# An attention-and-graph kernel on one core: the products with adj moved to stand behind the second block of queries, a pair's blocks dealt out anew among its four attention units, and the norms asked for one step sooner

## The chip, the core and the metric

The kernel runs on one core of a Trainium2 chip. The metric is the device time of one execution in microseconds (us). Before the change the median of three runs is 2553.65 us (2553.41 to 2556.24). The profile describes one execution with a span of 2553.1 us. The granted TensorE clock in it was 0.995 of full speed, so the clock plays no part in what follows.

## The reference

The input x has 64 graphs of 256 nodes with 512 features; adj is one 256 x 256 matrix of zeros and ones. Two layers follow each other, each a residual with a layer norm behind it:

```
def _L0_gnn_ref(x, adj, Wq, bq, Wk, bk, Wv, bv, Wo, bo):        # H = 8 heads of HD = 64
    q, k, v = (x @ W + b).reshape(b, n, H, HD) for each of the three
    scores = jnp.einsum('bqhd,bkhd->bhqk', q, k) / jnp.sqrt(jnp.float32(HD))
    scores = scores + (1.0 - adj)[None, None, :, :] * -1000000000.0
    attn = jax.nn.softmax(scores, axis=-1)
    out = jnp.einsum('bhqk,bkhd->bqhd', attn, v).reshape(b, n, d)
    return out @ Wo + bo
def _L1_gnn_ref(x, adj, weight, bias):
    y = jnp.einsum('nm,bmd->bnd', adj, x)
    return jnp.einsum('bnd,do->bno', y, weight) + bias

x = _layernorm(x + _L0_gnn_ref(x, adj, ...))
x = _layernorm(x + _L1_gnn_ref(x, adj, ...))
```

## The kernel before, in words

**Tiles.** The 64 graphs are worked through in 32 pairs. For each pair there are five large products with a 512 x 512 weight matrix: v, q and k (the values, queries and keys of attention), o (attention's output times Wo) and l (the second layer's output times its weight). Each is cut into four *blocks* of 128 x 512 (j = 0 to 3). To get float32-like accuracy from faster matmuls, both operands are split into three parts (high, low and a difference), and a block is three part products of four matmuls each. `near` (L317) does the first two parts into a PSUM bank and has ScalarE scale what stands there (L326); `far` (L328) does the third part later and has the bank emptied: for v, q, k by ScalarE (L347, L352), for o and l by VectorE, which adds it to the residual rows r (L338). There are four banks for these products (`ps_mm`, four buffers), and `LAGGED` (L522) holds the blocks that have had `near` but not `far`; `block` (L532) leaves at most two of them open, and the step `f1` or `f0` in the order below closes all but one, or all.

**Splitting the operands.** On VectorE, `chunk_parts` (L284) makes the parts of one 128-row chunk of the input of o or l: cut (L168), clow (L169) and cdiff (L174); ScalarE makes chigh from cut (L298). `x_t`, `x_parts` and `x_diff` (L240 to L274) do the same for the rows of x of a later pair, in xT, x, low and diff.

**Attention.** A pair has four *units*: two graphs times two groups of four heads. One `slot` (L580) finishes one unit and begins the next: `values` (L384) does row sums (L394) and attention times v (L402), which ScalarE takes out of PSUM as zc (L396) and vc (L405); `scores` (L359) does q times k for the next unit in two halves (kc = 0 and 1, L367), and ScalarE takes the exponential (L371). The PSUM tiles `at` of a slot are six, in a ring of four buffers: the second half of the scores goes into the buffers of zc's and vc's inputs.

**The products with adj.** `adj_x` (L501) multiplies adj with the normed rows; there are four for a pair (y0 to y3). Its input comes out of a chain: when `far` of o's last block has run, `norm` (L433) begins; ScalarE squares the rows (`squared`, L442), VectorE and GpSimd make the inverse roots (L446), VectorE makes `less` (L465), ScalarE norms the rows (`normed`, L476), and `halves` splits them into two parts hl on ScalarE and VectorE (L498, L499). The rows of the second layer pass through the same norm and go out to DRAM.

**What sets the order.** In the middle of the kernel (windows 1 to 30, one for each pair) the order of the instructions on TensorE, ScalarE and VectorE is exactly the order in which the Python code issues them (`manual_schedule`). `between` (L540) writes the large steps of a window by hand as one list, `seq`. The small steps of the norm chain are put off by `later(n, ...)` (L225): they are issued after n further *ticks*, and a tick comes after every block, slot and adj product (L591). In a window w, the blocks of o and l belong to the pair behind (w - 1), those of v, q and k to the pair ahead (w + 1), and the slots to the pair w. A window takes 77.4 us; this document calls its four slots S1 (which opens the window), S2, S3 and S4.

Of the kernel before, what the change touches and what calls it, by code (L numbers as in the profile page):

```python
# [43 lines left out]
def fast(tc, x, adj, wq, bq, wk, bk, wv, bv, wo, bo, w1, b1, out):  # L44
# [6 lines left out]
    NP = B // 2  # L51
# [78 lines left out]
    def raw_weight(name, tiles, queue):  # L130

        for i in range(3):
            SCRATCH[name, i] = scratch.tile([P, DC, D], F32, name=f"{name}{i}")
        n = DC // len(tiles)
        for i, t in enumerate(tiles):
            for k in range(n):
                RAW[name, i * n + k] = t[:, k]
            w = SOURCE[name][i * n * P:(i + 1) * n * P]
            if name == "o":


                for a in range(n):
                    queue.dma_start(t[:, a], w.rearrange("(h a i) e -> a h i e", h=4, a=2)[a])
            else:
                queue.dma_start(t, w.rearrange("(c p) e -> p c e", p=P))
# [79 lines left out]
    def later(n, f, *args):  # L225
        due.append([n, f, args])
# [101 lines left out]
    def far(name, p, j):  # L328
        pm = BANKS.pop((name, p, j))
        if (name, p, 2) in WP:  # L330
            part_product(pm, name, p, j, 2)
        b, c = divmod(j, 2)
        if name in "ol":
            r = R[p][b][:, c]
            if p < NP - 2:
                if j == 0:
                    ST[p, name] = small.tile([P, 4], F32, name="sums")
                nc.vector.scalar_tensor_tensor(r, pm, 1.0, r, op0=OP.mult, op1=OP.add, accum_out=ST[p, name][:, j:j + 1])  # L338
                if j == 3:
                    norm(p, name)  # L340
            else:
                nc.vector.tensor_tensor(r, r, pm, op=OP.add)
                norm_tile(p, name, j)
        elif name == "v":
            if c == 0:
                V[p, b] = four.tile([P, NC, D], F32, name="v")
            nc.scalar.activation(V[p, b][:, c], pm, AF.Copy)  # L347
        else:
            T, bias = (K, bk_s) if name == "k" else (Q, bq_s)
            if c == 0:  # L350
                T[p, b] = qk.tile([P, 2, 2, N], F32, name=name + "T")
            nc.scalar.activation(T[p, b][:, c].rearrange("p b i -> p (b i)"), pm, AF.Identity, bias=bias[:, j:j + 1])  # L352
# [80 lines left out]
    def norm(p, name):  # L433

        mean = small.tile([P, 4], F32, name="mean")
        nc.vector.tensor_scalar(mean, ST.pop((p, name)), -1 / D, None, op0=OP.mult)  # L436
        squares = small.tile([P, 4], F32, name="squares")
        for j in range(4):
            later(1 + j // 2, squared, p, j, mean, squares)
        later(3, inverse_roots, p, name, mean, squares)  # L440

    def squared(p, j, mean, squares):  # L442
        waste = one.tile([P, D], mybir.dt.bfloat16, name="z")
# [2 lines left out]
    def inverse_roots(p, name, mean, squares):  # L446
        nc.vector.tensor_scalar(squares, squares, 1 / D, EPS, op0=OP.mult, op1=OP.add)
        rstd = small.tile([P, 4], F32, name="rstd")
        nc.gpsimd.tensor_tensor(rstd, squares, power, op=OP.pow)
        later(1, less_of, p, name, 0, mean, rstd)  # L450

    def norm_tile(p, name, j):
        st = small.tile([P, nc.vector.BN_STATS_DIM], F32, name="st")
        nc.vector.bn_stats(st, R[p][j // 2][:, j % 2])
        mv = small.tile([P, nc.vector.BN_AGGR_DIM], F32, name="mv")
        nc.vector.bn_aggr(mv, st)
        ve = small.tile([P, 1], F32, name="ve")
        nc.vector.tensor_scalar(ve, mv[:, 1:2], EPS, None, op0=OP.add)
        rstd = small.tile([P, 1], F32, name="rstd1")
        nc.gpsimd.tensor_tensor(rstd, ve, power[:, 0:1], op=OP.pow)  # L460
        mean = small.tile([P, 1], F32, name="mean1")
        nc.vector.tensor_scalar(mean, mv[:, 0:1], -1.0, None, op0=OP.mult)
        later(1, less_of, p, name, j, mean, rstd)

    def less_of(p, name, j, mean, rstd):  # L465

        n = rstd.shape[1]
        less = small.tile([P, n], F32, name=f"less{n}")
        nc.vector.tensor_tensor(less, mean, rstd, op=OP.mult)  # L469
        for i in range(n):  # L470
            later(1 + i, normed, p, name == "l", j + i, rstd[:, i:i + 1], less[:, i:i + 1])

    def normed(p, layer, j, rstd, less):
        b, c = divmod(j, 2)
# [65 lines left out]
    def between(w):  # L540

        ahead, behind = w + 1, w - 1
        b = lambda name: [(block, name, behind if name in "ol" else ahead, j) for j in range(4)]
        v, q, k, o, l = (b(n) for n in "vqkol")
        c = lambda name, p: [(chunk_parts, name, p, j) for j in range(4)]
        y = [(adj_x, behind, i) for i in range(4)]
        bo_steps = [(with_bo, w, b) for b in range(2)]
        x_steps = [(x_t, w + 2, i) for i in range(4) if w + 2 < NP]
        x1 = [[s for f in (x_t, x_parts) for s in [(f, w + 2, i)] if w + 2 < NP] for i in range(4)]
        x2 = [[(x_diff, w + 2, i)] if w + 2 < NP else [] for i in range(4)]  # L550
        slot, f1 = [None], [(caught_up, 1)]
        f0 = [(caught_up,)]
        split = lambda name: [(split_w, name, i) for i in range(4)]
        mixed = lambda m, n: [s for pair in zip(m, n) for s in pair]
        halves_tiles = lambda: [one.tile([P, 2, D], F32, name=f"hl{i}") for i in range(2)]
        if w == -1:
            return [(x_t, 0, i) for i in range(4)] + mixed(v, split("v")) + mixed(q, split("q")) + [(adj_t,)] + \
                mixed(k, x_steps)
        if w == 0:
            raw_weight("o", halves_tiles(), nc.sync)  # L560
            PENDING[:] = [s for m, n in zip(x1, x2) for s in m + n]
            return slot + mixed(v, split("k")) + slot + q[:3] + split("o") + [(bv_wo,), (load_w, 3)] + \
                [(lambda: raw_weight("l", halves_tiles(), nc.sync),)] + slot + q[3:] + k[:2] + split("l") + \
                [(load_r, 0)] + slot + k[2:] + bo_steps + c("o", w)[:2] + \
                [(load_w, 3), (load_r, 1)]
        co, cl = c("o", behind), c("l", behind)
        seq = slot + co[2:3] + o[:1] + f1 + co[3:] + o[1:2] + PENDING[:6] + o[2:] + PENDING[6:] + slot + v + q[:1] + slot + q[1:] + f1 + \
            y[:1] + f0 + y[1:2] + k[:1] + (cl[:1] if w < NP - 2 else []) + y[2:] + f0 + bo_steps + slot + k[1:2] + \
            (cl[1:2] if w < NP - 2 else [])
        PENDING[:] = x1[3] + x2[3]  # L570
        if w == NP - 2:
            co = c("o", w)
            return seq + k[2:3] + co[:1] + k[3:] + co[1:2] + [(block, "o", w, 0)] + cl[:1] + [(block, "o", w, 1)] + cl[1:2]
        seq += k[2:3] + cl[2:3] + k[3:] + x1[0] + l[:1] + f1 + x2[0] + x1[1] + x2[1] + l[1:2] + cl[3:] + \
            l[2:3] + c("o", w)[:1] + x1[2] + x2[2] + l[3:] + f1 + c("o", w)[1:2]
        return seq

    PENDING = []
# [16 lines left out]
    def window(w):  # L595
        steps(between(w), [(w - 1, 3)] + [(w, u) for u in range(4)])
# [235 lines left out]
```

## Time and profile before

| engine | busy us | share of the span |
|---|---|---|
| TensorE (PE), matmuls | 2496.0 | 98% |
| TensorE weight loads (PEld) | 1886.6 | 74% |
| VectorE (DVE) | 1872.6 | 73% |
| ScalarE (ACT) | 1705.7 | 67% |
| GpSimd (POOL) | 382.4 | 15% |

Windows 2 to 29 repeat to within 0.02 us: the longest pieces of the chain of waits begin at 222.88, 300.26, 377.62, 455.00 us and so on, 77.38 us apart. In one such window (996.62 to 1074.00 us) TensorE is busy for 76.74 us, VectorE for 57.49 us and ScalarE for 53.09 us.

How to read a timeline: each line is one or more instructions of one engine with the start and the length in us, the line of the kernel, what it writes from what it reads, and in brackets the time that the engine stood idle ahead of it and what ended that. Matmuls overlap: four of them show as 1.07 us, but the next group starts 0.91 us after the first one did.

### The profile page before, as it was taken

What the parts mean: (1) busy time and instruction counts of PE and PEld (TensorE: products, weight loads), DVE (VectorE), ACT (ScalarE), POOL (GpSimd) and SP (SyncE); (2) the same over time, 40 slices, a digit from 0 to 9 for tenths busy, and PEclk for the clock granted to TensorE, in tenths of its full rate; (3) what the DMA queues carried; (4) which work ended last, traced back from release to release, by engine and by line L of the source; (5) the groups of instructions that cost most, each with busy time, mean ns of one, the idle gap of its engine ahead of it and who ended that gap; (6) DMA issues with size and microseconds to landing.
All of it is one profiled execution on the core that took longest, in us unless ns stands there. A gap on an engine that the chain in (4) does not pass through costs nothing.

```text
span 2553.1 us, 42184 instructions
## 1 busy us (share of the span) xinstructions
PE 2496.0 (98%) x15806; PEld 1886.6 (74%) x15806; DVE 1872.6 (73%) x3239; ACT 1705.7 (67%) x3206; POOL 382.4 (15%) x793
## 2 busy tenths in 40 slices
PE   8999999999999999999999999999999999999997
PEld 4477777777777777777777777777777777777765
DVE  4676787677886677876767876768876778866786
ACT  4557666776666766666776667766667766677755
POOL 0111111111111111111111111111111111111101
PEclk9999999999999999999999999999999999999998
DMA  7868778778788687777787787787787787777711
GB/s 205 284 201 273 235 232 259 240 244 243 240 256 247 236 263 232 235 250 252 231 274 226 232 259 243 240 262 234 246 246 247 251 247 233 247 254 229 257 68 51
DMA packets 375744, 600.25 MB, mean 235 GB/s; under 512 B 273520, under 2 KB 273776, under 8 KB 317552
## 3 DMA queue, kind: packets, MB, share of 16 engines
q0 software_dynamic: 65232, 475.03, 51.9%
q1 hardware_dynamic: 309760, 121.42, 22.0%
q8 instruction: 127, 2.08, 0.3%
q10 hardware_dynamic: 544, 1.05, 0.1%
q14 instruction: 81, 0.66, 0.1%
HBM read 548.15 MB, written 49.28 MB: 234 GB/s over the span
## 4 chain that ended last, share of the span: by engine, by line
PE 70%; DVE 25%; issue 3%; DMA 1%; ACT 0%; POOL 0%; SPq 0%; DVEq 0%; ACTq 0%
PE mm L314 50%; PE at L367 7%; PE at L402 6%; PE mm L512 5%; DVE clow L169 4%; DVE r L338 3%; DVE cdiff L174 3%; DVE diff L174 2%; DVE cut L168 2%; PE at L394 2%; DVE e L376 2%; DVE low L169 2%; DVE xT L264 2%; DVE x L168 1%; DVE o L418 1%
## 5 line engine op out<-in xcount | busy, mean ns | idle before, releaser
L326 ACT ACTIVATE mm<-mm 128x512 f32<-128x512 f32 x616 | 357.8, 581 | 356.7 <-PE mm L314 356.6
L376 DVE TENSOR_TENSOR e<-e,adjT 128x1024 f32<-128x1024 f32 x256 | 307.6, 1221 | 34.2 <-ACT e L371 34.2
L314 PE MATMUL mm<-wr,clow 128*128 128x512 f32 x1024 | 285.1, 401 | 25.1 <-DVE clow L169 24.6
L371 ACT ACTIVATE e<-at 128x512 f32<-128x512 f32 x512 | 265.2, 604 | 52.9 <-PE at L367 52.9
L314 PE MATMUL mm<-wr,chigh 128*128 128x512 f32 x1024 | 279.9, 396 | 0.7
L314 PE MATMUL mm<-wr,cdiff 128*128 128x512 f32 x1024 | 269.6, 391 | 5.9 <-ACT mm L326 5.9
L314 PE MATMUL mm<-low,wr 128*128 128x512 f32 x960 | 265.1, 398 | 0.0
L314 PE MATMUL mm<-high,wr 128*128 128x512 f32 x960 | 257.2, 390 | 0.0
L367 PE MATMUL at<-qT,kT 64*128 64x256 f32 x2048 | 256.6, 389 | 0.1
L314 PEld LDWEIGHTS mm<-wr,clow 128*128 128x128 f32 x1024 | 188.7, 190 | 86.6 <-DVE clow L169 38.3
L314 PE MATMUL mm<-diff,wr 128*128 128x512 f32 x960 | 248.5, 391 | 0.0
L402 PE MATMUL at<-e,v 128*32 128x256 f32 x4096 | 246.9, 381 | 0.0
L367 PEld LDWEIGHTS at<-qT,kT 64*128 64x128 f32 x2048 | 190.6, 186 | 67.7 <-issue 53.0
L499 DVE TENSOR_TENSOR hl<-r,hl 128x512 fp32r<-128x512 f32 x122 | 84.3, 691 | 203.4 <-ACT hl L498 203.4
L314 PEld LDWEIGHTS mm<-wr,chigh 128*128 128x128 f32 x1024 | 191.5, 189 | 53.0 <-ACT chigh L298 14.2
L314 PEld LDWEIGHTS mm<-wr,cdiff 128*128 128x128 f32 x1024 | 192.5, 188 | 48.1 <-ACT mm L326 7.8
L444 ACT ACTIVATE z<-r,mean 128x512 bf16<-128x512 f32 x240 | 172.6, 719 | 76.2 <-DVE mean L436 71.2
L314 PEld LDWEIGHTS mm<-low,wr 128*128 128x128 f32 x960 | 173.6, 188 | 51.6 <-issue 19.9
L338 DVE SCALAR_TENSOR_TENSOR r<-mm,r 128x512 f32<-128x512 f32 x240 | 160.4, 687 | 69.6 <-PE mm L314 69.6
L314 PEld LDWEIGHTS mm<-high,wr 128*128 128x128 f32 x960 | 180.3, 188 | 38.4
L476 ACT ACTIVATE r<-r,less,rstd 128x512 f32<-128x512 f32 x248 | 200.4, 808 | 6.1 <-DVE less L469 6.1
L314 PEld LDWEIGHTS mm<-diff,wr 128*128 128x128 f32 x960 | 176.3, 188 | 33.6
(123 smaller groups left out, 3985.0 us busy)
## 6 DMA issues: line engine op xcount, KB each, us to landing
wr<-o POOLq DMA_DIRECT2D x93, 1024.0 KB, 6.3
wr<-v POOLq DMA_DIRECT2D x90, 1024.0 KB, 6.4
wr<-q POOLq DMA_DIRECT2D x90, 1024.0 KB, 6.5
wr<-k POOLq DMA_DIRECT2D x90, 1024.0 KB, 7.3
wr<-l POOLq DMA_DIRECT2D x90, 1024.0 KB, 7.6
x<-in_x_dram SPq DMA_DIRECT2D x496, 64.0 KB, 6.4
r<-in_x_dram SPq DMA_DIRECT2D x31, 1024.0 KB, 5.3
out_dram<-r SPq DMA_DIRECT2D x60, 512.0 KB, 6.5
```

The costliest lines, as they stand in the source:

```text
L169: nc.vector.tensor_tensor(low, a, cut, op=OP.subtract)
L174: nc.vector.scalar_tensor_tensor(diff, low.bitcast(F32), -(FINE + 1), a, op0=OP.mult, op1=OP.add)
L314: nc.tensor.matmul(pm, *operands(name, p, j, i, k), start=k == 0 and i == begins, stop=k == DC - 1, skip_group_check=True)
L326: nc.scalar.activation(pm, pm, AF.Copy, scale=1 + 1 / FINE)
L338: nc.vector.scalar_tensor_tensor(r, pm, 1.0, r, op0=OP.mult, op1=OP.add, accum_out=ST[p, name][:, j:j + 1])
L367: nc.tensor.matmul(sc[s][:, a, :], K[p, g][r, a, b, kc * P:(kc + 1) * P], Q[p, g][r, a, b, :], start=True, stop=True)
L371: nc.scalar.activation(e[:, s], sc[s], AF.Exp, scale=qscale)
L376: nc.vector.tensor_tensor(e, e, mask[:, kc:kc + 1, :].to_broadcast([P, 4, N]), op=OP.mult)
L402: nc.tensor.matmul(at[h * 32:(h + 1) * 32, a, :], V[p, b][:, kc, col:col + 32], e[kc][:, h % 2, h // 2, :], start=kc == 0, stop=kc == NC - 1)
L444: nc.scalar.activation(waste, R[p][j // 2][:, j % 2], AF.Square, bias=mean[:, j:j + 1], accum_out=squares[:, j:j + 1])
L476: nc.scalar.activation(r, r, AF.Identity, scale=rstd, bias=less)
L512: nc.tensor.matmul(pm[:, j, :], hl[:, i, mc, j * P:(j + 1) * P], adjT[:, mc, :], start=mc == 0 and i == 0, stop=mc == NC - 1 and i == 1)
```

## The change

The change edits three places. No operation is added or removed; the order in which the code issues them is what differs, and with it the order on three engines.

- In `norm`, `inverse_roots` is put off by two ticks instead of three, and in `less_of` the four `normed` are put off by 1, 1, 2, 2 ticks instead of 1, 2, 3, 4. The rows are therefore issued for norming sooner.
- In `between`, the open blocks of o are closed around S2 (`f1` ahead of it, `f0` behind it), so that the norm of the pair begins ahead of v's first block instead of behind its second.
- Also in `between`, y0 and y1 now stand behind the second block of q and y2 and y3 between the third and the fourth, where they stood behind the fourth and around the first block of k; and the chunks 0, 1 and 2 of l's input (`cl`) are split ahead of S4, where chunks 1 and 2 were split behind it. The place of S2, S3 and S4 among the blocks' `near` parts stays: behind o, behind q's first block and behind k's first block.

The intent is to give the adj products and the splitting of their results to a part of the window in which VectorE has little to do.

```
-        later(3, inverse_roots, p, name, mean, squares)
+        later(2, inverse_roots, p, name, mean, squares)
...
-            later(1 + i, normed, p, name == "l", j + i, rstd[:, i:i + 1], less[:, i:i + 1])
+            later(1 + i // 2, normed, p, name == "l", j + i, rstd[:, i:i + 1], less[:, i:i + 1])
...
-        seq = slot + co[2:3] + o[:1] + f1 + co[3:] + o[1:2] + PENDING[:6] + o[2:] + PENDING[6:] + slot + v + q[:1] + slot + q[1:] + f1 + \
-            y[:1] + f0 + y[1:2] + k[:1] + (cl[:1] if w < NP - 2 else []) + y[2:] + f0 + bo_steps + slot + k[1:2] + \
-            (cl[1:2] if w < NP - 2 else [])
+        seq = slot + co[2:3] + o[:1] + f1 + co[3:] + o[1:2] + PENDING[:6] + o[2:] + PENDING[6:] + f1 + slot + f0 + v + q[:1] + slot + q[1:2] + f1 + \
+            y[:1] + f0 + y[1:2] + q[2:3] + (cl[:2] if w < NP - 2 else []) + y[2:3] + f0 + y[3:] + q[3:] + \
+            (cl[2:3] if w < NP - 2 else []) + k[:1] + bo_steps + slot + k[1:2]
...
-        seq += k[2:3] + cl[2:3] + k[3:] + x1[0] + l[:1] + f1 + x2[0] + x1[1] + x2[1] + l[1:2] + cl[3:] + \
+        seq += k[2:] + x1[0] + l[:1] + f1 + x2[0] + x1[1] + x2[1] + l[1:2] + cl[3:] + \
             l[2:3] + c("o", w)[:1] + x1[2] + x2[2] + l[3:] + f1 + c("o", w)[1:2]
```

## The prediction

> **What bounds the kernel now.** I read the page's busy times first, then its chain of waits, then the waits of the repeating middle part (200 to 2350 us), then one window's timeline.
>
> ```profile
> PE 2496.0 (98%) x15806; PEld 1886.6 (74%) x15806; DVE 1872.6 (73%) x3239; ACT 1705.7 (67%) x3206; POOL 382.4 (15%) x793
> ...
> PE 70%; DVE 25%; issue 3%; DMA 1%; ACT 0%; POOL 0%; SPq 0%; DVEq 0%; ACTq 0%
> ```
>
> TensorE is the bound, yet a quarter of the chain lies on VectorE: somewhere TensorE waits for a long run of VectorE work. The middle's waits (in all, times, longest, in us) name the place:
>
> ```profile
> PEld mm L314 <- DVE clow L169: 28.8, 28, 1.0
> ...
> PE mm L314 <- DVE clow L169: 17.0, 28, 0.6
> ...
> DVE diff L174 <- PE mm L314: 8.6, 26, 0.3
> ```
>
> TensorE's matmuls have one wait a window and no other: for clow. The timeline shows that it is the last chunk of o, just after S1 (o's fourth block, o3):
>
> ```profile
> 1064.74 1.07 PE L314 MATMUL mm<-wr,cdiff 128*128 128x512 f32 x4
> ...
> 1065.67 0.69 DVE L169 TENSOR_TENSOR clow<-o,cut 128x512 fp32r<-128x512 f32 x1
> ...
> 1066.42 0.76 PEld L314 LDWEIGHTS mm<-wr,clow 128*128 128x128 f32 x4 [1.03 <-DVE clow L169]
> 1066.42 1.20 PE L314 MATMUL mm<-wr,clow 128*128 128x512 f32 x4 [0.61 <-DVE clow L169]
> ...
> 1067.65 0.75 PEld L314 LDWEIGHTS mm<-wr,chigh 128*128 128x128 f32 x4 [0.47 <-ACT chigh L298]
> ```
>
> Groups of four matmuls follow each other every 0.907 us. From 1064.74 four groups and the 0.1 us ahead of a slot would put S2 at 1068.47; it is at 1069.69. The wait thus costs 1.22 us a window. It stands at the head of windows 2 to 30: 29 x 1.22 = 35.4 us. Nothing else is to be had in the middle: 60 groups x 0.907 = 54.4, four slots x 4.45 = 17.8, the adj products 3.9, and 1.22 make 77.3 of the 77.38 us.
>
> **Where VectorE falls behind.** VectorE has no idle time to speak of from 1028 to 1074 us, which suggests too much work ahead of o3. But two places inside tie it to TensorE:
>
> ```profile
> 1044.29 0.69 DVE L169 TENSOR_TENSOR low<-xT,x 128x512 fp32r<-128x512 f32 x1
> 1045.31 0.69 DVE L174 SCALAR_TENSOR_TENSOR diff<-low,xT 128x512 fp32r<-128x512 f32 x1 [0.33 <-PE mm L314]
> ...
> 1050.52 0.69 DVE L338 SCALAR_TENSOR_TENSOR r<-mm,r 128x512 f32<-128x512 f32 x1
> ```
>
> The first diff of x must wait until k3's `far`, begun at 1044.88, has read the buffer that it overwrites: VectorE is 0.33 us too early there, in every window. The r at 1050.52 waits for `far` of l0, which begins at 1049.42 and takes 1.07 (1050.49). From there to the end of clow at 1066.36 VectorE works without a wait: 15.84 us. TensorE needs 1049.42 to 1065.65 from the same l0 to the point where it wants clow. So the stall is made wholly between l0's `far` and o3.
>
> **What the Trainium skill says.** "Perfetto Trace Analysis", Identifying the Most-Contended Engine: TensorE's matmul busy share is no measure of headroom; here it is 98%, and the waits give the 1.4% that can be won. The same page, Optimization Strategy: a gap that repeats on the engine that should be saturated can mean too few buffers. This one repeats every 77.38 us, but the trace ends it with clow, so it is late work. "TensorE: Matmul & The Clock Gate", Architectural detail: ScalarE and VectorE are strict FIFO, and TensorE can pull weight loads ahead of running matmuls; the trace agrees (VectorE stands 0.33 us at diff with ready work behind it; a load begins 0.23 us ahead of its matmul). So one late item delays all behind it on ScalarE and VectorE. Prices for ScalarE are below.
>
> **The change, part by part.** The built order of both programs shows what moves.
>
> *Chunks 1 and 2 of l ahead of S4.* This takes 2 x (0.42 + 0.69 + 0.69) = 3.6 us (start to start) of VectorE's work out of the stretch behind S4. But it stood ahead of the first diff. VectorE will only arrive there earlier and wait longer: two more `far` groups now stand behind S4 (q3's and k0's), so k3's `far` itself comes 1.8 us later after S4. From that diff through o3 the three manual orders (TensorE, VectorE, ScalarE) have the same instructions in the same sequence before and after. Expected gain: 0. The 1.22 us stay.
>
> *Norm of l sooner.* `inverse_roots` of l now stands on VectorE behind o0's r, so o1's and o2's additions wait for squares and for GpSimd's 1.04 us (rstd). This is behind the clow of o3. Their banks are wanted by v1 and v2, from 6 us after S2 on; I reckon the additions done by 3. Cost 0.
>
> *f1 ahead of S2, f0 behind it.* A group of 0.907 us moves from one side of v0 to the other. Cost 0.
>
> *ScalarE between S2 and S3.* The norm work that had room till y0 is now packed ahead of S3. Step lengths start to start, from the timeline: scaling 0.52, v out 0.48, normed 0.70, two squares 1.57, hl 0.52.
>
> ```profile
> 1086.12 0.58 ACT L347 ACTIVATE v<-mm 128x512 f32<-128x512 f32 x1
> 1086.60 0.80 ACT L476 ACTIVATE r<-r,less,rstd 128x512 f32<-128x512 f32 x1
> 1087.30 0.58 ACT L326 ACTIVATE mm<-mm 128x512 f32<-128x512 f32 x1
> ...
> 1088.46 0.38 ACT L396 ACTIVATE zc<-at 128x256 f32<-128x256 f32 x1
> 1090.19 0.60 ACT L405 ACTIVATE vc<-at 128x512 f32<-128x512 f32 x1 [1.34 <-PE at L402]
> ```
>
> The skill's "ScalarE: Activation LUTs", What ACT_TABLE_LOAD costs, prices an ACTIVATE of N elements at 186 + 0.833 N ns, 93 more for each pointer operand, with 93 of overlap: for normed (two pointers) 799 - 93 = 706 ns; the trace has 0.70 us.
>
> Two places can bite. (1) q0 needs v0's bank. After S2's exponentials (ScalarE free at S2 + 5.38) come 2 normed (6.78), v0's scaling (not ready before 7.3, so 7.82), 2 normed (9.22), 2 squares (10.79), scaling (11.31), 2 squares (12.88), scaling (13.40), v0 out, done at 13.98. TensorE wants the bank at S2 + 4.22 + 1.03 + 10 groups = 14.32. Margin 0.3: cost 0, at worst 0.2. (2) S3 itself. `far` of v2 starts 1.00 us ahead of S3, its result is ready 1.11 us later, at S3 + 0.11. Then v2 out (0.48), 2 normed (1.40) and hl (0.52) put zc at S3 + 2.51, where it was at 0.70; zc takes 0.28 to 0.38 ahead of vc, which needs 0.60: done at S3 + 3.39 to 3.49. The second half of the scores writes into vc's buffer with the tenth of 16 matmuls: they run from S3 + 2.29 to 4.22, so the tenth is due at 3.38. A release takes 0.06 (clow's end 1066.36 to 1066.42). New wait: 0.07 to 0.17 us a window, at worst 0.4 if ScalarE is later than I think, at best 0 if it is a little quicker. I take 0.1. Behind the waiting matmul stand the other seven score matmuls and q1; TensorE pays it in full.
>
> *adj products sooner.* y0 is due at S3 + 4.34 + 4 groups = S3 + 8.0; its hl is ready near S3 + 3.3, and hl1 follows ScalarE's exponentials near S3 + 6.7: no wait. y2 and y3 find their hl some 2 us ready. In the trace y0, y1 and y2+y3 last 0.94, 1.04 and 1.89; split into four the sum is 3.87 to 4.0: 0 to 0.1 us more, I take 0.05. Weight loads: q, k and l are asked for over 10 us ahead of use against a landing time of 6.3 to 7.6 us: 0.
>
> Sum: 30 windows x (0.10 + 0.05) = +4.5 us; bounds 30 x 0 and 30 x 0.5. 2553.65 + 4.5 = 2558.
>
> **The rivals.** *Faster, 2521:* VectorE's head start of 3.6 us reaches o3, and the stall goes: -35.4 + about 3. For it: the stall is VectorE's, 3.6 exceeds 1.22, and VectorE sits idle for much of 1081 to 1100. Against: the wait at diff, and an unchanged 15.84 us behind l0's `far`. Half of it would give 2540. *Slower by much, 2568 to 2585:* ScalarE's queue ahead of S3 costs 0.5 to 1 us a window, because v0's bank also comes late or GpSimd's rstd holds the first normed (and all behind it). For it: four operations stand between v2's result and zc, and the margins are tenths of a microsecond. Against: ScalarE has slack of 0.3 us ahead of v2's result, which takes up small delays. *Hidden, 2554:* both small costs are zero and only the stall stays.
>
> **How the numbers follow.** Main case (stall kept, 0 to 8 us added, the hidden case in it): 0.70, of which 0.44 within 0.2% (5.1 us) and 0.26 beyond. Faster rival 0.16. Much slower 0.14. So faster 0.16, same 0.44, slower 0.40. The range 2550 to 2578 takes in the main case and over half of the slower rival; about 0.2 is left out.
>
> **What would show it.** Right: o3's wait for clow is there with 0.61 us; the wait of diff for PE is longer than 0.33 us, by several; zc starts about 2.5 us after S3, and a short wait at L367 for ACT vc appears. Wrong: the clow line is gone or shorter with S2 nearer to S1, or PE waits at L314 for ACT v, or long ones at L512 for hl.

## The result, and the profile after

| | median us | lowest to highest | runs |
|---|---|---|---|
| before | 2553.87 | 2553.41 to 2556.24 | 4 |
| after | 2564.17 | 2561.14 to 2566.96 | 4 |

The ratio is 1.0038, with a 95% interval of 1.0021 to 1.0056: the changed kernel is 10.3 us (0.4%) slower. The prediction, 2558, had the direction of its small costs right and about half of their size.

The page of the changed kernel, busy times and then the shares of the chain of waits. It looks like that of before: TensorE is busy for 12 us more, in a span that is 12 us longer, so its share is the same.

```profile
PE 2507.9 (98%) x15806; PEld 1895.5 (74%) x15806; DVE 1874.5 (73%) x3239; ACT 1711.5 (67%) x3206; POOL 390.7 (15%) x793
...
PE 70%; DVE 25%; issue 3%; DMA 1%; ACT 1%; SPq 0%; POOL 0%; DVEq 0%; ACTq 0%
```

A quarter of the chain is still VectorE's. The waits of the middle part (200 to 2350 us; in all, times, longest) say what stayed and what is new:

```profile
DVE diff L174 <- PE mm L314: 128.2, 27, 4.8
...
PEld mm L314 <- DVE clow L169: 28.7, 28, 1.0
DVE low L169 <- PE mm L314: 25.2, 27, 0.9
...
PE mm L314 <- DVE clow L169: 16.9, 28, 0.6
...
PEld at L367 <- PE at L402: 11.5, 28, 0.4
...
PE at L367 <- ACT zc L396: 1.6, 1, 1.6
```

The 0.4 us of the weight loads at L367 is not new: before has the same 0.41 at S3, there with no releaser named. The low ahead of the first diff of x now waits for TensorE, 0.9 us a window. The main thing is this: TensorE's wait for clow is what it was, 16.9 us in 28 times, against 17.0, and VectorE's wait at the first diff of x was 8.6 us in all and is 128.2. The timeline of one window shows both. On TensorE, at o3 behind S1:

```profile
1069.06 1.07 PE L314 MATMUL mm<-wr,cdiff 128*128 128x512 f32 x4
...
1069.99 0.69 DVE L169 TENSOR_TENSOR clow<-o,cut 128x512 fp32r<-128x512 f32 x1
...
1070.73 0.76 PEld L314 LDWEIGHTS mm<-wr,clow 128*128 128x128 f32 x4 [1.02 <-DVE clow L169]
1070.73 1.20 PE L314 MATMUL mm<-wr,clow 128*128 128x512 f32 x4 [0.60 <-DVE clow L169]
...
1071.96 0.76 PEld L314 LDWEIGHTS mm<-wr,chigh 128*128 128x128 f32 x4 [0.47 <-ACT chigh L298]
```

and on VectorE some 20 us ahead of it:

```profile
1049.63 0.69 DVE L174 SCALAR_TENSOR_TENSOR diff<-low,xT 128x512 fp32r<-128x512 f32 x1 [4.75 <-PE mm L314]
```

VectorE stands still for 4.75 us in every window, and 20 us later TensorE waits 0.60 us (weight load 1.02 us) for VectorE, as before. So the time gained for VectorE is there, but in front of the tie and not behind it.

The windows view gives a window from its start in us, then its length and each engine's busy time in it (PE, PEld, DVE, ACT, POOL):

```profile
996.62:1074.32 77.70, 77.07 (x497) 59.42 (x497) 57.53 (x99) 53.27 (x101) 12.44 (x25) 1.00 0.81 243
```

The steady windows have become 77.69 us long, where they were 77.38. That no TensorE wait of its own appears for the 0.31 us is the first thing to explain. The starts of the slots' row sums (L394) in the traces, subtracted from each other, say where they lie (us; the typical steady window of each kernel, which single ones miss by some hundredths; the one window with a long wait, told of below, is left out):

| kernel | S2 to S3 | S3 to S4 | S4 to S1 | S1 to S2 | window |
|---|---|---|---|---|---|
| before | 18.05 | 21.08 | 22.60 | 15.65 | 77.38 |
| after | 17.14 | 19.60 | 24.39 | 16.55 | 77.69 |

Most of this is work that changed sides. The `far` groups last 0.907 us each. One went from behind S2 to ahead of it, two from ahead of S4 to behind it. That gives 17.14, 19.27, 24.41 and 16.56. Only S3 to S4 misses this, by 0.33 us. Inside it the timeline finds S3 itself. ScalarE, with S3's row sums begun at 1092.05:

```profile
1090.27 1.52 ACT L476 ACTIVATE r<-r,less,rstd 128x512 f32<-128x512 f32 x2 [0.24 <-DVE less L469]
1091.70 0.58 ACT L326 ACTIVATE mm<-mm 128x512 f32<-128x512 f32 x1
1092.22 0.58 ACT L347 ACTIVATE v<-mm 128x512 f32<-128x512 f32 x1
1092.69 1.50 ACT L476 ACTIVATE r<-r,less,rstd 128x512 f32<-128x512 f32 x2
1094.10 0.61 ACT L498 ACTIVATE hl<-r 128x512 fp32r<-128x512 f32 x1
1094.62 0.36 ACT L396 ACTIVATE zc<-at 128x256 f32<-128x256 f32 x1
1094.88 0.58 ACT L405 ACTIVATE vc<-at 128x512 f32<-128x512 f32 x1
```

TensorE and its weight loads in the same slot:

```profile
1092.05 0.64 PE L394 MATMUL at<-sm,ones 128*32 128x256 f32 x8
1092.50 1.91 PE L402 MATMUL at<-e,v 128*32 128x256 f32 x32
1094.34 2.30 PE L367 MATMUL at<-qT,kT 64*128 64x256 f32 x16
...
1094.34 1.90 PEld L367 LDWEIGHTS at<-qT,kT 64*128 64x128 f32 x16 [0.41 <-PE at L402]
```

zc starts 2.57 us behind S3's start and vc ends 3.41 behind it. The 16 score matmuls (the trace shows each of the code's eight as two) last 2.30 us and their weight loads 1.90. In the kernel before, at the same slot (its S3 begins at 1087.76), they last 2.00 and 1.60:

```profile
1090.05 1.60 PEld L367 LDWEIGHTS at<-qT,kT 64*128 64x128 f32 x16 [0.41 <-issue]
1090.05 2.00 PE L367 MATMUL at<-qT,kT 64*128 64x256 f32 x16
```

A window of 0.01 us around 1095.51 shows the one load of the changed kernel that came late. It starts 0.05 us after vc's end:

```profile
1095.51 0.18 PEld L367 LDWEIGHTS at<-qT,kT 64*128 64x128 f32 x1
```

The wait is inside the group. The waits view of the middle names no matmul of L367 waiting for vc, because the pause in front of one matmul is shorter than the modelled length of the one still running. The group's length shows what the waits don't.

### The profile page after: what moved, and what is told of

Read it like the earlier page. It is cut to its first block, busy times and chain, and to the rows that moved or that the text cites. A ratio compares the mean times of both kernels' runs of the same rounds, so it can differ in the third digit from the quotient of the medians.

```text
span 2565.2 us, 42038 instructions
## 1 busy us (share of the span) xinstructions
PE 2507.9 (98%) x15806; PEld 1895.5 (74%) x15806; DVE 1874.5 (73%) x3239; ACT 1711.5 (67%) x3206; POOL 390.7 (15%) x793
## 4 chain that ended last, share of the span: by engine, by line
PE 70%; DVE 25%; issue 3%; DMA 1%; ACT 1%; SPq 0%; POOL 0%; DVEq 0%; ACTq 0%
PE mm L314 49%; PE at L367 7%; PE at L402 6%; PE mm L512 5%; DVE clow L169 4%; DVE r L338 3%; DVE cdiff L174 3%; DVE diff L174 2%; DVE cut L168 2%; PE at L394 2%; DVE e L376 2%; DVE low L169 2%; DVE xT L264 2%; DVE x L168 1%; DVE o L418 1%
## 5 line engine op out<-in xcount | busy, mean ns | idle before, releaser
L314 PE MATMUL mm<-wr,clow 128*128 128x512 f32 x1024 | 283.9, 399 | 23.7 <-DVE clow L169 23.2
L314 PE MATMUL mm<-wr,chigh 128*128 128x512 f32 x1024 | 279.4, 395 | 0.8
L314 PE MATMUL mm<-wr,cdiff 128*128 128x512 f32 x1024 | 267.6, 393 | 6.7 <-ACT mm L326 6.7
L367 PE MATMUL at<-qT,kT 64*128 64x256 f32 x2048 | 266.7, 391 | 1.6 <-ACT zc L396 1.6
L314 PE MATMUL mm<-low,wr 128*128 128x512 f32 x960 | 265.9, 399 | 1.3 <-ACT v L347 1.3
L314 PE MATMUL mm<-high,wr 128*128 128x512 f32 x960 | 258.2, 391 | 0.0
L314 PE MATMUL mm<-diff,wr 128*128 128x512 f32 x960 | 254.8, 392 | 0.0
L367 PEld LDWEIGHTS at<-qT,kT 64*128 64x128 f32 x2048 | 198.6, 186 | 71.4 <-issue 40.7
L314 PEld LDWEIGHTS mm<-wr,clow 128*128 128x128 f32 x1024 | 187.7, 189 | 85.3 <-DVE clow L169 37.7
L314 PEld LDWEIGHTS mm<-wr,cdiff 128*128 128x128 f32 x1024 | 189.5, 188 | 56.9 <-issue 9.9
L314 PEld LDWEIGHTS mm<-wr,chigh 128*128 128x128 f32 x1024 | 190.9, 189 | 53.0 <-ACT chigh L298 14.3
L314 PEld LDWEIGHTS mm<-low,wr 128*128 128x128 f32 x960 | 171.4, 188 | 51.7 <-issue 19.9
L314 PEld LDWEIGHTS mm<-high,wr 128*128 128x128 f32 x960 | 180.2, 188 | 39.5
L314 PEld LDWEIGHTS mm<-diff,wr 128*128 128x128 f32 x960 | 175.8, 188 | 33.5
L476 ACT ACTIVATE r<-r,less,rstd 128x512 f32<-128x512 f32 x248 | 188.6, 811 | 15.7 <-DVE less L469 15.7
L402 PEld LDWEIGHTS at<-e,v 128*32 128x32 f32 x4096 | 133.5, 110 | 88.5 <-issue 1.3
```

The costliest lines, as they stand in the source:

```text
L314: nc.tensor.matmul(pm, *operands(name, p, j, i, k), start=k == 0 and i == begins, stop=k == DC - 1, skip_group_check=True)
L367: nc.tensor.matmul(sc[s][:, a, :], K[p, g][r, a, b, kc * P:(kc + 1) * P], Q[p, g][r, a, b, :], start=True, stop=True)
L402: nc.tensor.matmul(at[h * 32:(h + 1) * 32, a, :], V[p, b][:, kc, col:col + 32], e[kc][:, h % 2, h // 2, :], start=kc == 0, stop=kc == NC - 1)
L476: nc.scalar.activation(r, r, AF.Identity, scale=rstd, bias=less)
```

## The experiments

The theory after the result: the steady loss is S3's late release by ScalarE (0.31 us a window), and the stall at o3 is set by VectorE's work behind l0's `far`, so nothing that stands ahead of the tie can shorten it. Rivals: that the norms cost time by being sooner; that splitting chunks of l's input elsewhere costs or gains by itself; and that the loss lies in the adj products now split into four. Each experiment is timed against the kernel before on the same chip (2553.90 to 2556.03 us there); the changed kernel was not timed again beside them. "Window" is worked out from the slots' starts as above, and the waits of the middle are those of 200 to 2300 us.

### e1: S3 without the split of the rows in its way

In the changed kernel, the two `halves` of a pair of rows are both put off by two ticks, so that the first hl is issued behind S3 instead of ahead of it. Nothing else differs.

```
-                later(1 + half, halves, p, b, half)
+                later(2 if p < NP - 2 else 1 + half, halves, p, b, half)
```

> The changed kernel with both first splits of the normed rows (hl) issued one step later, behind the exponentials of S3 instead of ahead of zc. Theory: the changed kernel's loss of 0.31 us a window is ScalarE's queue ahead of zc and vc in S3; without hl there, vc ends 0.52 us sooner (near S3 + 2.9), the score matmuls of S3 run in 1.93 us again, and S3 to S4 falls from 19.60 to 19.3 us: about 29 x 0.3 = 9 us less than the changed kernel, 2555. Rival (the loss is in splitting the adj products into four, or in the norms as a whole): S3 to S4 stays at 19.6 and the time at 2564.

Measured: 2554.29 us against 2556.03, ratio 0.9992 (0.9984 to 1.0000). The window is 77.37, S3 to S4 19.29. ScalarE and TensorE at S3, which begins at 698.30 here:

```profile
698.95 1.50 ACT L476 ACTIVATE r<-r,less,rstd 128x512 f32<-128x512 f32 x2
700.35 0.36 ACT L396 ACTIVATE zc<-at 128x256 f32<-128x256 f32 x1
700.74 0.60 ACT L405 ACTIVATE vc<-at 128x512 f32<-128x512 f32 x1
701.76 2.07 ACT L371 ACTIVATE e<-at 128x512 f32<-128x512 f32 x4 [0.43 <-PE at L367]
703.69 1.17 ACT L498 ACTIVATE hl<-r 128x512 fp32r<-128x512 f32 x2
```

```profile
698.30 0.64 PE L394 MATMUL at<-sm,ones 128*32 128x256 f32 x8
698.76 1.91 PE L402 MATMUL at<-e,v 128*32 128x256 f32 x32
700.60 2.00 PE L367 MATMUL at<-qT,kT 64*128 64x256 f32 x16
```

zc starts 2.05 behind S3's start and vc ends 3.04 behind it, and the 16 score matmuls take 2.00 us again. One ScalarE operation of 0.52 us moved behind the slot wins back the whole 0.31 us of the window. So the steady loss is S3's. The adj products stand in four single pieces here too and the 0.31 us is gone, so that rival falls.

### e4: the norms sooner, alone

In the kernel before, only the two lines that put the norm off less.

```
-        later(3, inverse_roots, p, name, mean, squares)
+        later(2, inverse_roots, p, name, mean, squares)
...
-            later(1 + i, normed, p, name == "l", j + i, rstd[:, i:i + 1], less[:, i:i + 1])
+            later(1 + i // 2, normed, p, name == "l", j + i, rstd[:, i:i + 1], less[:, i:i + 1])
```

> The kernel before with the two edits of the norms alone (inverse roots two steps behind, normed at 1, 1, 2, 2). The products with adj and the closing of o's blocks stay. Theory: only the first two normed stand ahead of zc in S3 and ScalarE has slack there, so nothing moves: 2554 within 3 us, S3 to S4 stays at 21.08 us. Rival (asking for the norms sooner is itself what costs): 9 to 12 us more, near 2564.

Measured: 2551.87 against 2556.03, ratio 0.9986 (0.9980 to 0.9993); the window is 77.27. Norms sooner cost nothing by themselves, and this part of the change even gains a little: 0.08 us of the 0.11 lie between S3 and S4, where the adj product y1 takes 0.94 us instead of 1.03. At e4's S3 two `normed` stand ahead of zc and no split hl; zc starts at S3 + 2.01 and vc ends at 3.03, as before. What does harm is the hl in front of S3 as well, and it gets there only with the earlier `f0`; no run has that `f0` alone.

### e2 and e3: two chunks ahead of the tie, on both kernels

The chunk 3 of l's input and chunk 0 of o's are split ahead of l0's addition r instead of behind it, and their chigh is issued at once. On after (e2; e3 does the same to the list of before):

```
-        seq += k[2:] + x1[0] + l[:1] + f1 + x2[0] + x1[1] + x2[1] + l[1:2] + cl[3:] + \
-            l[2:3] + c("o", w)[:1] + x1[2] + x2[2] + l[3:] + f1 + c("o", w)[1:2]
+        now = lambda name, p, j: [(chunk_high, name, p, j)]
+        seq += k[2:] + x1[0] + l[:1] + cl[3:] + now("l", behind, 3) + f1 + x2[0] + x1[1] + x2[1] + l[1:2] + c("o", w)[:1] + now("o", w, 0) + \
+            l[2:3] + x1[2] + x2[2] + l[3:] + f1 + c("o", w)[1:2]
```

> The changed kernel with two chunks of VectorE's work moved within the stretch that ends at o3: l's chunk 3 goes ahead of the first diff of x, where VectorE waits for k3's far product, and o's chunk 0 goes ahead of the addition that waits for l0's far product. Theory: the stall at o3 is made behind l0's far product, so taking cut and clow (1.18 us) from there removes most of the 1.0 us of waiting: 1.0 to 1.2 us a window, 29 to 35 us, so 2530 to 2535. Rival (VectorE as a whole is too late, or ScalarE's chigh is what counts): the wait for clow stays at 0.6 us and the time at 2564.

> The same move of the two chunks in the kernel before. There VectorE reaches the first diff only 0.33 us ahead of TensorE and l0's addition 0.08 us ahead, so it has no idle time in which to do the moved work. Theory that the room counts: at most 0.4 us a window is gained, 0 to 12 us: 2542 to 2554, and it may lose where diff comes later. Rival (the order alone counts, and the change made no room that matters): 29 to 35 us less, about 2520.

Measured: e2 2526.58 against 2556.03, ratio 0.9882 (0.9866 to 0.9897), window 76.50, a little better than expected; e3 2544.61, ratio 0.9956 (0.9943 to 0.9970), window 77.07 (three of its windows are 0.35 longer). The waits of the middle, e2:

```profile
DVE clow L169 <- PE mm L314: 64.0, 27, 2.4
...
DVE cdiff L174 <- PE mm L314: 17.5, 27, 0.7
DVE diff L174 <- PE mm L314: 16.8, 27, 0.6
...
PE at L367 <- ACT zc L396: 1.6, 1, 1.6
```

and e3:

```profile
PEld mm L314 <- DVE clow L169: 22.2, 31, 1.1
...
PE mm L314 <- DVE clow L169: 9.4, 28, 0.6
```

In e2 no matmul of L314 waits for clow any more; the direction is turned round, and VectorE waits for TensorE (2.4 us at a clow, 0.7 at a cdiff). In e3 the stall is cut from 17.0 us in all to 9.4. The edit is the same, but the room is not: before leaves VectorE 0.33 us of idle time ahead of the tie, and the window shrinks by 0.31; after leaves 4.75, and the window shrinks by 1.19, nearly the whole loss of 1.22. So the tie is where the prediction put it, and the change does make something that can be used: idle time on VectorE in the right place, which it doesn't fill. (The edit moves the two chunks and issues their chigh at once; the two parts were not tried apart.)

### e6, e7 and e8: the chunks moved, alone

e6 puts the chunks 1 and 2 of l's input ahead of S4 in the kernel before, without the rest of the change.

```
-            y[:1] + f0 + y[1:2] + k[:1] + (cl[:1] if w < NP - 2 else []) + y[2:] + f0 + bo_steps + slot + k[1:2] + \
-            (cl[1:2] if w < NP - 2 else [])
+            y[:1] + f0 + y[1:2] + k[:1] + (cl[:1] if w < NP - 2 else []) + y[2:] + f0 + (cl[1:3] if w < NP - 2 else []) + bo_steps + slot + k[1:2]
...
-        seq += k[2:3] + cl[2:3] + k[3:] + x1[0] + l[:1] + f1 + x2[0] + x1[1] + x2[1] + l[1:2] + cl[3:] + \
+        seq += k[2:] + x1[0] + l[:1] + f1 + x2[0] + x1[1] + x2[1] + l[1:2] + cl[3:] + \
```

> The kernel before with one part of the change alone: l's chunks 1 and 2 are split ahead of S4 instead of behind it. Theory: VectorE's head start of 3.6 us is spent waiting at the first diff of x; that wait grows from 0.33 us to about 3 us and more, the wait for clow at o3 stays at 0.6 us, and the time stays within 3 us of the kernel before. Rival (VectorE's lateness behind S4 is what makes the stall): the clow wait goes and the time falls by about 35 us.

e7 is e6 with the edit of e3 added.

> The kernel before with l's chunks 1 and 2 ahead of S4 and with the two chunks moved within the stretch that ends at o3. Theory: the first move makes room, the second uses it: 1.0 to 1.2 us a window less than before, 2519 to 2525, though each alone gives 0 and 11 us. Rival (the adj products' new place is needed for the room): no more than the 11 us of the early chunks alone, 2545.

Measured: e6 2663.42 against 2554.07, ratio 1.0429 (1.0414 to 1.0443); e7 2662.14, ratio 1.0420 (1.0405 to 1.0434). Both expectations missed by over 100 us. The waits of e6:

```profile
DVE cut L168 <- ACT chigh L298: 98.1, 26, 3.8
...
PEld mm L314 <- ACT chigh L298: 95.8, 37, 3.6
PE mm L314 <- DVE clow L169: 86.7, 33, 3.2
```

There is one buffer for `cut`. The chigh that reads it is put off by a tick, and in e6 no tick stands between the two chunks. So chunk 1's chigh is issued behind the slot, behind S4's exponentials on ScalarE, and chunk 2's cut waits 3.8 us for it on VectorE, with everything behind it. This is made by the experiment's own order: in the changed kernel y2, y3 and q3 stand between the two chunks. e7 carries the same wait and says nothing of its question.

e8 mends it by issuing chigh right behind each chunk (shown against e6; the line that defines `now` is left out):

```
-            y[:1] + f0 + y[1:2] + k[:1] + (cl[:1] if w < NP - 2 else []) + y[2:] + f0 + (cl[1:3] if w < NP - 2 else []) + bo_steps + slot + k[1:2]
+            y[:1] + f0 + y[1:2] + k[:1] + (cl[:1] if w < NP - 2 else []) + y[2:] + f0 + (cl[1:2] + now(1) + cl[2:3] + now(2) if w < NP - 2 else []) + bo_steps + slot + k[1:2]
```

> The kernel before with l's chunks 1 and 2 ahead of S4, as in the run that lost 109 us, but with each chunk's chigh issued on ScalarE right behind its cut, so that the single cut buffer is free again ahead of S4. Theory: the 109 us came from chunk 2's cut waiting for chunk 1's chigh, which stood behind S4's exponentials; without it the move changes nothing that TensorE waits for, since VectorE is busy on both sides of S4 and its wait at the first diff of x stays near 0.33 us: 2554 within 5 us, clow wait 0.6 us. Rival (VectorE's bo additions and S4's work being later is what cost): still far above, 2600 or more.

Measured: 2583.40 against 2553.90, ratio 1.0112 (1.0096 to 1.0127). Eighty of the 109 us are gone, so the wait at cut was their cause; but 29.5 are left, where 0 were expected. They lie at S4: S4 to S1 is 23.54 where before has 22.60, the other spacings are those of before. The waits of e8:

```profile
DVE diff L174 <- PE mm L314: 30.3, 26, 1.2
...
PE mm L314 <- DVE clow L169: 16.3, 27, 0.6
PEld at L367 <- ACT zc L396: 15.8, 26, 0.6
...
PE at L367 <- ACT zc L396: 5.3, 26, 0.2
PEld at L367 <- ACT vc L405: 5.0, 26, 0.2
```

Two chigh stand ahead of S4's zc and vc on ScalarE now, and the score matmuls wait for the buffers of both. That is the mechanism of S3 in a second place, made by accident and three times as dear (0.94 us a window). TensorE's wait for clow is the same 0.6, so the chunks' move alone doesn't shorten the stall. Nor does it make room: VectorE's wait at diff is 1.2 us instead of 0.3, and the 0.9 between them is what S4 delays TensorE. In this order VectorE works without a wait from ahead of the moved chunks up to that diff, so moving them only changes the sequence of its work.

### e9 and e10: the changed kernel with the chunks back in their old place

e9 takes only the moved chunks out of the change, in the other direction: chunks 1 and 2 stand behind S4 again.

```
-            y[:1] + f0 + y[1:2] + q[2:3] + (cl[:2] if w < NP - 2 else []) + y[2:3] + f0 + y[3:] + q[3:] + \
-            (cl[2:3] if w < NP - 2 else []) + k[:1] + bo_steps + slot + k[1:2]
+            y[:1] + f0 + y[1:2] + q[2:3] + (cl[:1] if w < NP - 2 else []) + y[2:3] + f0 + y[3:] + q[3:] + \
+            k[:1] + bo_steps + slot + k[1:2] + (cl[1:2] if w < NP - 2 else [])
...
-        seq += k[2:] + x1[0] + l[:1] + f1 + x2[0] + x1[1] + x2[1] + l[1:2] + cl[3:] + \
+        seq += k[2:3] + cl[2:3] + k[3:] + x1[0] + l[:1] + f1 + x2[0] + x1[1] + x2[1] + l[1:2] + cl[3:] + \
```

> The changed kernel with l's chunks 1 and 2 put back behind S4, where they stood before. Theory: this takes 3.6 us of VectorE's idle time at the first diff of x (4.7 us in the changed kernel, so about 1.1 us left) and nothing that TensorE waits for: clow wait 0.6 us, S3 to S4 at 19.6 us, time 2564 as the changed kernel within 4 us. Rival (the chunks' new place does shorten the stall in part): slower by some 10 us or more, 2575 and up.

e10 is e9 with the edit of e2.

> As the last one, with l's chunk 3 and o's chunk 0 moved ahead within the stretch that ends at o3. Theory: what is gained is bounded by VectorE's idle time at the first diff of x: 0.33 us of it gave 0.31 us a window in the kernel before, 4.7 us gave 1.19 us (all there was). With about 1.1 us of it the gain should be 0.9 to 1.19 us a window, 26 to 35 us below the run without the early chunks: 2529 to 2538. Rival (the room does not matter in the changed order): 2528 as with the chunks ahead of S4, or no gain.

Measured: e9 2564.53 against 2553.90, ratio 1.0039 (1.0026 to 1.0053), the spacings within 0.02 us of those of after, window 77.70; e10 2545.82, ratio 0.9971 (0.9960 to 0.9981), window 77.01. The waits of e9:

```profile
DVE cut L168 <- ACT chigh L298: 36.9, 27, 1.4
...
DVE diff L174 <- PE mm L314: 17.6, 27, 0.7
...
PE mm L314 <- DVE clow L169: 16.4, 27, 0.6
```

The place of the chunks is worth nothing by itself: with them in front of S4 the window is 77.69, behind it 77.70. It only decides how much idle time VectorE has at diff: 4.75 us, or 0.65. The latter was expected at about 1.1, and with it e10's time was expected 8 to 17 us lower. The reckoning had left out the 0.94 us that VectorE also stands at the low ahead of that diff in the changed kernel: 4.75 + 0.94 - 3.6 = 2.1, and e9 has 1.37 of it at cut, waiting for chigh, and 0.65 at diff. The chunks that e10 moves stand behind that cut, so they can use only the 0.65. The stall lies between S1 and S2, and there e10's gain, 16.55 - 15.91 = 0.64, is again the room. Three pairs lie side by side:

| kernel without and with the early chunks | idle of VectorE at the first diff, us | S1 to S2 shorter by, us |
|---|---|---|
| before and e3 | 0.33 | 0.31 |
| e9 and e10 | 0.65 | 0.64 |
| after and e2 | 4.75 | 1.18 (the stall costs 1.22) |

In e10's steady windows no matmul is listed as waiting for clow any more, yet S1 to S2 is 0.54 us longer than in e2 (15.91 against 15.37). Here too the spacing shows a loss that the list of waits leaves out.

### e5: both repairs

The changed kernel with e1's and e2's edits, and o's last chigh issued right behind its chunk:

```
+        ... + co[3:] + now("o", behind, 3) + o[1:2] + ...
```

> The changed kernel with both repairs: the hl splits behind the exponentials of S3, and the two chunks moved within the stretch that ends at o3 (besides, chigh of o's chunk 3 is issued ahead of the squares). Theory: the two losses are in different places and simply add: 0.31 us a window less than the run with the early chunks alone, so about 76.18 us a window and 2517 to 2519. Rival (one takes up the other's gain): no better than 2526.

Measured: 2519.00 us against 2554.07, ratio 0.9862 (0.9847 to 0.9877); window 76.13. It beats the kernel before by 35 us, and the changed kernel's time above by 45. In the middle part one TensorE wait for another engine's result is left in front of a matmul, in one window:

```profile
PE at L367 <- ACT zc L396: 1.1, 1, 1.1
```

The prediction put the stall's price at 35.4 us in all, and about 35 came back. From e1 to e5, S1 to S2 falls from 16.55 to 15.33 us, by the stall's whole 1.22. Of the split between the two repairs, e2 gives 76.50 and e5 76.13: of the 0.37 us between them 0.33 lies between S3 and S4, the S3 loss, and 0.04 between S1 and S2, where e5 alone issues o's last chigh sooner.

## Why the prediction was right or wrong

**What bounds the kernel: right.** The stall at o3 is real time and worth what was worked out: 1.22 us a window, 1.18 of which e2 takes away between S1 and S2, and e5 all.

**The stall stays: right.** TensorE's wait is 0.60 us (0.61), its load's 1.02 (1.03). The reason given, that VectorE is tied to TensorE behind l0's `far` and that earlier work ends in a longer wait at the first diff, is what e2, e3, e9 and e10 show: moving work across that tie gains just what room there is, and moving it about ahead of the tie gains nothing. The wait at diff, "longer by several", grew from 0.33 to 4.75 us. With the 0.94 at the low ahead of it VectorE stands 5.69 us there, which is about what the prediction's parts add up to: the old 0.33, the 3.6 of the two chunks and the 1.8 by which k3's `far` comes later.

**The faster rival: wrong as the change stands.** Its 2521 is the time of e5 (2519), but only with two chunks moved across the tie, from behind it into VectorE's idle time, and one hl out of S3's way. The change makes the room and does not use it.

**The costs taken as zero: right.** The norm of l on VectorE, v0's bank for q0, the weight loads and hl for y0 to y3 show no wait in the steady windows. ScalarE's slack ahead of v2's result took up the delay of rstd: the first of the late `normed` waits 0.24 us for less, and v2 still comes out at 0.17 us behind S3's start. The adj products in four pieces were put at 0.05 us a window, and this may be about right: e1, which has them, comes to 77.37, but it has the sooner norms as well, and those alone give 77.27 (e4). The 0.10 lies between S3 and S4, where e1's `far` between y2 and y3 takes 0.98 us from start to start instead of 0.91 and the two groups behind y3 0.93 and 0.92. So up to 0.1 for the split and as much gained by the norms seem to cancel; no run has the split alone. The price from the Trainium skill's "ScalarE: Activation LUTs", What ACT_TABLE_LOAD costs, held: two `normed` and the step to hl take 1094.10 - 1092.69 = 1.41 us, 0.705 each, for an estimate of 0.706.

**ScalarE at S3: the place and the queue right, the deadline wrong.** zc was put at S3 + 2.51 and is at 2.57; vc's end was put at 3.39 to 3.49 and is at 3.41. The step that failed is "so the tenth is due at 3.38". It spaced the 16 matmuls evenly, one behind another. In the records they run in pairs, one matmul on each 64-row half of the array, with starts 5 to 8 ns apart and a pair every 0.215 us (0.32 behind the first). The second half of the scores begins with a pair, so the tenth matmul starts together with the ninth, at S3 + 3.27 when nothing is late, and its weights are loaded at 3.08. That load is what has to wait for vc's buffer. In the kernel before, vc ended at 3.03 and the load followed 0.05 later, just in time. In the changed kernel vc ends at 3.41 and the load starts at 3.47, its matmul with it. From there on this half of the array stays behind (its last matmul starts at 4.22 instead of 3.92), while the other half keeps its times. So the wait costs 0.30 us (2.30 - 2.00 for the group) instead of 0.10. That is within the 0 to 0.4 that the prediction allowed for it; but the sign that it named, a wait at L367 for vc, is not listed in the steady windows. The Trainium skill has the reason for the pairs in "TensorEngine Tiling (Array Packing)", Tiling Modes: the array can be two tiles of 64 x 128 (Available Configurations), and different tiles can load weights and multiply in parallel (Key Properties). The records agree (the starts 5 to 8 ns apart). The even spacing of the prediction could have been avoided: the single starts in one slot of the trace of before show the pairs.

**The sum.** 0.10 + 0.05 a window was predicted, 4.5 us in all. At S3 it is 0.31, and 29 x 0.31 = 9.0 us, while the 0.05 does not show on balance. So the term of S3's wait was put at a third of its size. The measured 10.3 lies above the main case's 0 to 8 and below the slower rival's 2568; the range of 2550 to 2578 holds it. The profiled executions differ by 12.1 us, which can be added up, but for rounding, from the starts of their first and last slots: 9.0 from the windows, 2.0 from one single wait (below), 0.7 more between the first and the last slot that I did not follow, 2.0 ahead of the first slot, and 1.7 less behind the last, not followed either. The 2.0 ahead of the first slot is no part of the change: e9 has the same beginning as after and its first slot at 69.9 us, where after has 72.9 and before 70.8.

**What the prediction did not have: a pause of GpSimd.** In the profiled execution of after there is one S3 at which TensorE waits 1.58 us for zc. The timeline around it, over all engines (lines of other engines left out):

```profile
1245.87 0.54 POOL L127 DMA_DIRECT2D wr<-k  x1 [9.25 <-issue]
1246.42 1.04 POOL L449 TENSOR_TENSOR rstd<-squares,power 128x4 f32<-128x4 f32 x1
...
1247.49 0.17 DVE L469 TENSOR_TENSOR less<-mean,rstd 128x4 f32<-128x4 f32 x1 [2.95 <-POOL rstd L449]
1247.69 1.52 ACT L476 ACTIVATE r<-r,less,rstd 128x512 f32<-128x512 f32 x2 [2.26 <-DVE less L469]
```

GpSimd issues nothing for 9.25 us ahead of one weight load, rstd stands behind that load in its queue, and less, `normed` and zc are late one after the other. The kernel before has such a pause too, 5.60 us at 1240.92, and TensorE doesn't notice it. In e1, e2, e5, e9 and e10, which have the change's order, the pause is again 9.25 us, between 1224 and 1245 us, and one wait for zc of 1.1 to 1.6 us follows; e3 and e4, with the order of before, have 5.60 and 5.62 and no such wait. The kernels with the change's order have a second pause, 4.3 to 4.4 us ahead of a load of q's weights between 683 and 695 us, which TensorE doesn't notice. I read it so: with the norm's chain packed ahead of S3, its slack no longer covers the pause. No run moved the pause or the load, so that is argued, not shown, and why the pause is longer stays open; at 2 us in 2564 it matters little. It is the rival's "GpSimd's rstd holds the first normed", true in one window of thirty.

## What to carry to other kernels

Ahead of moving work to an engine that is late, find the last place before the stall where that engine itself waits for the engine that stalls: only work that crosses this tie can gain, and in the three pairs here it gained as much as the engine stood idle there, up to the stall. When operations are packed ahead of a slot on an in-order engine, reckon the deadline of the buffer they hold back from single instruction starts (the weight load, and side-by-side matmuls) and not from an even spacing; in this kernel a deadline put 0.3 us too late (3.38 for a load due at 3.08) was the difference between noise and a loss. An idle stretch that a change leaves on a wanted engine can be worth a gain later: e5 fills it, takes the hl out of S3's way, and turns 10 us lost into 35 won.

## What the runs showed of the hardware

- Score matmuls of 64 rows on the two halves of the array start 5 to 8 ns apart, and such pairs follow each other every 0.215 us, the second 0.32 behind the first. When the weight load of one half is held back, that half does not catch up and the other half keeps its times: 2.30 us instead of 2.00 for 16.
- A matmul group can lose 0.3 us to another engine with no wait shown in front of it; the group's length, the weight loads' total (1.90 against 1.60 us) and the slots' spacing show it.
- GpSimd pauses ahead of issuing a weight load near the middle of an execution, with nothing in the trace that it waits for: 5.59 to 5.62 us in the six kernels with the order of before, 9.25 us in the six with the change's order, which have another pause of 4.3 to 4.4 us near 690 us. The lengths repeat to a few hundredths of a microsecond on three chips, so they go with the order of the program and are not chance.
